# A graph layer with expert routing: two groups of seven node tiles in place of one of fourteen, and the first nodes' maxima moved behind them

## The chip, the cores and the metric

The kernel runs on one core of a Trainium2 chip. The metric is device time in microseconds (us), the median over repeated executions; lower is better. Five engines work side by side, each in the order of its own program: PE (matrix products; its weight loads are listed apart as PEld), DVE (vector operations), ACT (activations and copies; it also issues DMAs), POOL (here it issues the indirect DMAs, one row index per partition) and SP (it issues DMAs). They wait for each other and for transfers by semaphores.

## The reference, cut to what matters

There are 3125 nodes with 256 features (25 tiles of 128 nodes) and 100000 edges, sorted by destination. In outline:

```
xn  = layernorm(x)
a   = xn @ theta.T ;  b = xn @ (phi - theta).T          # per node
gnn = max over edges e of node d: relu(a[d] + b[src[e]] + biases)
mix = linear attention over all nodes: q (k^T v / N) w_out + b_out
x   = x + gnn + mix
# mixture of 8 experts, the best 2 of each node
x   = x + sum of 2: weight * (gelu(layernorm(x) @ W1[e]) @ W2[e])
```

All arithmetic is float32; an expert's two weight matrices are 2 MB together. Low node numbers have many edges: the 16 first nodes get a share of theirs by another way, told below.

## The kernel before, in words

**Head.** All 25 tiles are normalized and transposed, and `b` is written to a table in DRAM (L244 to L268). A search finds where each node's edges end.

**Edges.** The edges, from the highest node down, are laid out over 128 partitions and four stages of `STEPS` = 263, 209, 157 and 98 columns, 727 in all. For each column POOL issues one gather of 128 rows of `b` (L112, 1 KB a row) into a window of 8 columns; there are 5 windows (`wide`, `WN`). DVE folds column by column into a running maximum (`fold`, L387), and SP stores each finished window to a table `s_d` (L1487), after which the window can be filled again. A stage belongs to a group of node tiles: `GROUPS` = tiles 11 to 24, 4 to 10, 1 to 3, and 0.

**After a stage** (`group`, L1293): `carry` (L390) sends the last column through PE, a DVE scan and PE again, so that a run of edges that crosses partitions gets its maximum. Then for each tile POOL fetches the nodes' maxima from `s_d` (L416) and `token_tile` (L443) adds what belongs together, normalizes, and computes the routing logits on PE. `dispatch` (L1270) ranks the tokens and POOL scatters each tile twice to the experts' rows in `xs_d` (L119). Then the group joins the expert stream.

**Expert stream** (`Stream`, L682). A pass runs all 8 experts over a group. For tiles 11 to 24 every expert has room for `CAPS` = 512 rows, worked in two lots of 256; for tiles 4 to 10 it is one lot of 256, for tiles 1 to 3 one of 128. A lot is 8 steps of `hp` products (L645), a gelu on ACT (L647) and `yp` products (L669). Weights have three places; `plan` (L771) reuses those still there from the pass before and has ACT issue the others, in quarters of 512 KB between the steps. Tile 0 takes all its experts densely at the end (`dense_tile`), and `combine` (L1420) fetches the experts' rows back and writes the output.

**Work beside the edges.** `mixer` (L1163) handles one tile of the attention; 25 of them run under the first stage, after `turned` (L1100) has computed `b` transposed into `bT`. `without_edges` (L419) computes each tile's `a` and attention output. `first_nodes` (L1065) counts for each of the 16 first nodes which source nodes occur in the last 55 columns, and `first_maxima` (L1120) takes for each of them the maximum over all 25 tiles: PE spreads the node's mask (0 or -1e38) over 128 partitions into a PSUM bank (L1132), DVE adds it to `bT` and takes the maximum (L1136), for two halves of the features. It works on eight tiles (1024 columns) a step while the large bank is there, then on four (512) in a single bank that it shares with the expert stream.

**Order.** Every task is a Python generator; a clock that ticks once with each indirect DMA that POOL is given decides when its next piece is emitted, and `yield n` waits n ticks. PE, DVE, ACT and SP work in the order in which pieces were emitted. So a piece that comes late on one engine holds up everything emitted behind it there. `PER_TILE` and `PER_MIX` are the ticks between tiles. The mixers start at tick 16 but wait for `turned`, which starts at tick 30 and takes 21; `open_late` (L1246) frees the first part's memory and starts the expert stream, here at the end of the first stage's edges.

Of the kernel before, what the change touches and what calls it, by code (L numbers as in the profile page):

```python
# [8 lines left out]
F32 = mybir.dt.float32  # L9
# [25 lines left out]
ORDERS = ((0, 1, 2, 3, 4, 5, 6, 7), (6, 7, 5, 4, 0, 1, 2, 3), (2, 3, 1, 0, 4, 5, 6, 7))  # L35
# [6 lines left out]
GROUPS = ((11, 25), (4, 11), (1, 4), (0, 1))  # L42
STEPS = (263, 209, 157, 98)
CAPS = (512, 256, 128)
LOT = (256, 256, 128)
PARTS = (2, 2, 1)
# [14 lines left out]
PER_TILE = (5, 7, 4)  # L61
PACE = 0.9
# [10 lines left out]
def gps_layer(ctx: ExitStack, tc: tile.TileContext, x, src, dst, thetaT, phiT, gbias, wq, wkvT,  # L73
# [8 lines left out]
    clock = {"now": 0.0, "edges": 0, "tasks": 0, "pe": 0.0}  # L82

    def on_pe(us):
        clock["pe"] = max(clock["pe"], clock["now"]) + us / TICK

# [55 lines left out]
    bT = flat[:, 0:2 * NP].rearrange("p (h n) -> p h n", h=2)  # L142
    of_ring = ring.rearrange("p k n -> p (k n)")
    most = flat[:, 2 * NP:2 * NP + 2 * FIRST * CHUNKS].rearrange("p (h k c) -> p h k c", h=2, k=FIRST)
    ends_of = flat[:, 2 * NP + 2 * FIRST * CHUNKS:2 * NP + 2 * FIRST * (CHUNKS + 1)].rearrange("p (h k) -> p h k", h=2)
    halves = [of_ring[:, k * NP // 2:(k + 1) * NP // 2] for k in range(2)]
    no_edge = halves[1][0:FIRST].bitcast(BF16)
    unread = halves[0].bitcast(BF16)
# [39 lines left out]
    SPLIT = GROUPS[0][0]  # L188
    xn_lo = keep.tile([P, SPLIT, D], F32, name="xn_lo")
    xn_hi = keep.tile([P, NT - SPLIT, D], F32, name="xn_hi")  # L190
# [19 lines left out]
    row_of = keep.tile([FIRST, FIRST], BF16, name="row_of")  # L210
# [7 lines left out]
    nc.vector.tensor_copy(row_of, ident[0:FIRST, 0:FIRST])  # L218
# [171 lines left out]
    def carry(pool, ps, g, last, chain, carried):  # L390

        lt_p = ps.tile([P, 2, P], F32, name="mm")
        for c in range(2):
            nc.tensor.transpose(lt_p[:, c, :], last[:, c * P:(c + 1) * P], ident)
        on_pe(0.7)
        yield 3 if g < G - 1 else 1
        st = pool.tile([P, 2, P], F32, name="ct", bufs=2)
        for c in range(2):
            nc.vector.tensor_tensor_scan(st[:, c, :], through[:, g, :], lt_p[:, c, :],  # L399
                                         chain[0][:, c, P - 1:P] if chain else 0.0, op0=OP.add, op1=OP.max)  # L400
        chain[:] = [st]
        yield 2 if g < G - 1 else 1
        cr_p = ps.tile([P, D], F32, name="mm")
        for c in range(2):
            nc.tensor.transpose(cr_p[:, c * P:(c + 1) * P], st[:, c, :], ident)
        on_pe(0.7)
        yield 3 if g < G - 1 else 1
        cr = pool.tile([P, D + 1], F32, name=f"cr{g}", bufs=1)
        nc.vector.memset(cr[:, D:D + 1], 1.0)
        nc.vector.tensor_copy(cr[:, 0:D], cr_p)  # L410
        carried[g] = cr
# [7 lines left out]
    def without_edges(ps, i):  # L419

        am = ps.tile([P, 2 * D], F32, name="mm")
# [7 lines left out]
        nc.scalar.copy(x_sb[:, i, :], am[:, D:2 * D])  # L429

# [12 lines left out]
    def token_tile(work, ps, i, r1, slices, carried, top, top_i, newton=False, then=None,  # L443
# [56 lines left out]
        yield after(3)  # L500
        tr = ps.tile([P, 2, P], F32, name="mm")
# [5 lines left out]
        nc.scalar.copy(xtT, tr)  # L507
        yield after(2)
        lg = ps.tile([P, E], F32, name="mm")
# [6 lines left out]
        nc.vector.max_index(top_i, top, lg)  # L516

# [22 lines left out]
    def slots(ro, ps, g, half, i0, i1, pick, taken, chosen=None):  # L540
# [7 lines left out]
        if i1 == NT:  # L548
            nc.vector.tensor_scalar(took[:, nt - 1, :], took[:, nt - 1, :], real, None, op0=OP.mult)
        cnt_p = ps.tile([P, 2, nt, E], F32, name="mm")  # L550
# [20 lines left out]
        nc.vector.tensor_tensor(rank, cnt_p[:, 0], upto.rearrange("p e i -> p i e"), OP.add)  # L571

# [109 lines left out]
    class Stream:  # L682
# [9 lines left out]
        def add(self, g):  # L692
            self.lots += [(g, e, h) for e in ORDERS[g] for h in range(CAPS[g] // LOT[g])]

        def at_pair(self, u):

            g, e, h = self.lots[u]
            return h if CAPS[g] > LOT[g] else e % 2

        def half(self, u):  # L700

            g = self.lots[u][0]
            return LOT[g] // PARTS[g]

        def two(self, what, v):
# [3 lines left out]
            rows = what[g][e * CAPS[g]:e * CAPS[g] + 2 * LOT[g]]  # L709
            return rows.rearrange("(k p s) d -> p k s d", p=self.half(2 * v), k=2 * LOT[g] // CAPS[g])  # L710

        def at(self, to):

            return xn_hi[:, 4 * to:4 * to + 4, :]

        def as_two(self, rows, v):
            g = self.lots[2 * v][0]
            of = rows[0:self.half(2 * v), 0:2 * PARTS[g], :]
            return of.rearrange("p (k s) d -> p k s d", k=2 * LOT[g] // CAPS[g])
# [4 lines left out]
        def rows(self, v):  # L724
            if 2 * v < len(self.lots) and ("xs", v) not in self.held and not self.on_chip(2 * v):
                xs = self.held["xs", v] = self.at(v % 2)
                move(nc.scalar, self.as_two(xs, v), self.two(xs_d, v))
# [12 lines left out]
        def turn(self, u):  # L740
# [11 lines left out]
            elif ("xs", u // 2) in self.held and ("tr", u) not in self.held:  # L752
                tr = self.held["tr", u] = self.ps.tile([P, 2, ROWS], F32, name="trf", bufs=1)
                n = self.half(u)
                for c in range(2):
                    for r in range(2):
                        nc.tensor.transpose(tr[:, c, r * n:(r + 1) * n],  # L757
                                            self.held["xs", u // 2][0:n, self.at_pair(u) * 2 + r, c * P:(c + 1) * P],
# [3 lines left out]
        def scaled(self, u):  # L762
            if ("tr", u) in self.held and ("xe", u) not in self.held:
                e = self.lots[u][1]
                xe = self.held["xe", u] = self.act.tile([P, 2, ROWS], F32, name="xe")
                for c in range(2):
                    n = LOT[self.lots[u][0]]
# [30 lines left out]
        def more_w(self):  # L798
            while "firsts" not in clock:
                yield 1  # L800
            for k in (-2, -1):
                self.next_w(k)
                yield 25

        def go(self):
# [5 lines left out]
            while True:  # L811
                if u == len(self.lots):
# [3 lines left out]
                    units.behind = None  # L816
                    if not self.open:
# [13 lines left out]
                g, e, h = self.lots[u]  # L831
                v = u // 2
                if u % 2 == 0:
                    ys = self.at(2) if v % 2 else self.act.tile([P, 4, D], F32, name="ys", bufs=1)

                def done(r, yp, u=u, ys=ys):
                    g, e, h = self.lots[u]
                    n = self.half(u)
                    nc.tensor.matmul(yp[0:n, :], ident[0:E, e:e + 1].to_broadcast([E, n]), b2_sb, start=False, stop=True)  # L839
                    nc.scalar.copy(ys[0:n, self.at_pair(u) * PARTS[g] + r, :], yp[0:n, :])  # L840
                    if u % 2 and r == PARTS[g] - 1:
                        move(nc.scalar, self.two(ys_d, u // 2), self.as_two(ys, u // 2))
# [8 lines left out]
                if h == 0:  # L851
                    q += 1
                    if q:
                        between[7] = lambda q=q: (self.next_w(q, self.parts), self.part())
# [10 lines left out]
            dense_half(0, 1, xn_hi[:, 0:FC, :].rearrange("p i d -> p (i d)"), nc.scalar)  # L865
# [9 lines left out]
    def dense_tile(act, ps, mm, i, shared, w, next_w, order=range(E), ready=None):  # L875
# [5 lines left out]
        xT = act.tile([P, 2, P], F32, name="xT", bufs=1)  # L881
# [15 lines left out]
        o = act.tile([P, D], F32, name="o", bufs=1)  # L897
# [84 lines left out]
    p2 = early.enter_context(tc.tile_pool(name="p2", bufs=2, space=PSUM))  # L982
    column = ea.tile([P, FIRST * NT], I16, name="column")
# [4 lines left out]
    def loads():  # L988
# [19 lines left out]
        for g, cap in enumerate(CAPS):  # L1008
# [3 lines left out]
            n = LOT[g] // 2  # L1012
# [46 lines left out]
    def banks():  # L1059

        if "ffp" in at_hand:
            return 1, at_hand["ffp"].tile([P, 2, ROWS], F32, name="trf", bufs=1).rearrange("p c n -> p (c n)")
        return 2, p3.tile([P, 4 * ROWS], F32, name="banks")

    def first_nodes():  # L1065
# [10 lines left out]
        count_p = banks()[1][:, 0:FIRST * NT]  # L1076
# [9 lines left out]
        counts = ea.tile([P, FIRST, NT], F32, name="counts")  # L1086
        nc.scalar.copy(counts.rearrange("p k i -> p (k i)"), count_p)
        yield 2
        for i0 in range(0, NT, CHUNK):
            n = min(CHUNK, NT - i0)  # L1090
            rows_p = banks()[1][0:FIRST].rearrange("k (i p) -> k i p", p=P)
            for i in range(n):
                nc.tensor.transpose(rows_p[:, i, :], counts[:, :, i0 + i], ident)
            yield 2
            nc.vector.tensor_scalar(no_edge[:, i0 * P:(i0 + n) * P], rows_p[:, 0:n, :].rearrange("k i p -> k (i p)"), 0.5,
                                    NEG, op0=OP.is_lt, op1=OP.mult)
            yield 1
        start(first_maxima())

    def turned():  # L1100

        for i0 in range(0, NT, CHUNK):
            n = min(CHUNK, NT - i0)
            for h in range(2):
                bt_p = p2.tile([P, CHUNK, P], F32, name="k")
                for at, of, j, some in spans(i0, n):
                    for c in range(2):
                        nc.tensor.matmul(bt_p[:, at:at + some, :], wb[:, c, h * P:(h + 1) * P],  # L1108
                                         of[:, j:j + some, c * P:(c + 1) * P], start=(c == 0), stop=(c == 1))
                yield 1.5  # L1110
                nc.scalar.copy(bT[:, h, i0 * P:(i0 + n) * P], bt_p[:, 0:n, :].rearrange("p i n -> p (i n)"))
        clock["turned"] = True

    def spans(i0, n):

        low = max(0, min(n, SPLIT - i0))
        return [(at, of, j, some) for at, of, j, some in ((0, xn_lo, i0, low), (low, xn_hi, i0 + low - SPLIT, n - low))
                if some]

    def first_maxima():  # L1120

        nc.vector.memset(most, NEG)
        for k in range(FIRST):
            i0 = 0
            while i0 < NT:
                held, mask_p = banks()
                clock["bank"] = True
                tiles = min(held * CHUNK, NT - i0)
                n = tiles * P
                for at in range(0, n, CHUNK * P):  # L1130
                    to = min(n, at + CHUNK * P)
# [559 lines left out]
```

## Time and profile before

| | us |
|---|---|
| median of 14 runs (1697.84 to 1737.87) | 1711.21 |
| profiled execution | 1719.15 |
| its span, first to last instruction | 1717.3 |
| busy: PE / DVE / ACT / POOL | 1050.8 / 757.6 / 332.2 / 844.6 |
| 727 gathers of `b` on POOL (L112) | 702.9 |
| 723 folds on DVE (L387) | 349.1 |
| maxima of the first nodes on DVE (L1136): 78 of 1024 columns | 94.8 |
| the same: 36 of 512 columns | 24.5 |
| mean granted clock of PE, share of full | 0.752 |

Read it so: no engine is busy all the time, so the time is made of engines that wait for each other, stage by stage. "Granted clock" is the part of PE's full clock that the throttle left it. A row of the table by stage has the stretch, its length, and for each engine the busy time and the number of instructions; a row of the waits has who waited for what, the sum in us, how often, and the longest. "Remote" and "issue" stand for a release that the profile can't name.

### The profile page before, as it was taken

The numbers are of one execution on the slowest core, as the hardware profiler recorded it, in microseconds if no ns is written. First come the engines' busy times: TensorE is split into PE (matmuls) and PEld (weight loads), VectorE is DVE, ScalarE is ACT, GpSimd is POOL, SyncE is SP. The second block draws the span as 40 slices with busy tenths as digits, with TensorE's granted clock in tenths as the row PEclk, the third lists the DMA queues.
The fourth block names the chain that finished last, engine by engine and source line by source line (L and its number), as shares of the span: only waits on it lengthen the run. The fifth ranks groups of instructions, "written<-read, shape, count | busy, mean of one in ns | idle before, by whom it ended". The sixth has DMA issues, their size and how long they took to land.

```text
span 1717.3 us, 13741 instructions
## 1 busy us (share of the span) xinstructions
PE 1050.8 (61%) x4086; PEld 715.7 (42%) x4086; DVE 757.6 (44%) x2261; ACT 332.2 (19%) x796; POOL 844.6 (49%) x879
## 2 busy tenths in 40 slices
PE   3503866875584255731494996697025985479595
PEld 2401433332231133221373784575014864368484
DVE  3545776879559494323102103463331002515242
ACT  1300221221010121110121321221002322224131
POOL 6273573656645666377324434525771154631522
PEclk7755997887686555765696997788556996779696
DMA  7442663546446355255164654423651773549372
GB/s 234 154 148 77 232 230 129 184 164 204 160 146 238 120 204 187 92 202 165 51 216 132 230 197 153 153 111 138 205 187 37 250 236 101 196 138 354 121 268 79
DMA packets 93534, 292.88 MB, mean 171 GB/s; under 512 B 19398, under 2 KB 39871, under 8 KB 82698
## 3 DMA queue, kind: packets, MB, share of 16 engines
q0 software_dynamic: 42400, 115.28, 22.0%
q1 hardware_dynamic: 25420, 106.30, 16.0%
q10 hardware_dynamic: 25630, 70.34, 12.0%
q8 instruction: 34, 0.56, 0.1%
q14 instruction: 50, 0.41, 0.1%
HBM read 171.08 MB, written 120.75 MB: 170 GB/s over the span
## 4 chain that ended last, share of the span: by engine, by line
PE 40%; another core or an unknown queue 26%; DVE 15%; issue 14%; ACT 2%; DMA 2%; POOL 1%; ACTq 0%; DVEq 0%; SPq 0%; POOLq 0%
PE hp L645 12%; PE yp L669 11%; DVE g L387 4%; DVE ring L1136 2%; PE v L1168 2%; PE k L1168 2%; PE mm L424 2%; PE yp L839 2%; PE bp L262 2%; PE k L1108 1%; PE banks L1132 1%; ACT ring L647 1%; PE mm L422 1%; PE am L466 1%
## 5 line engine op out<-in xcount | busy, mean ns | idle before, releaser
L112 POOL DMA_INDIRECT g<-b_d,srcI x727 | 702.9, 967 | 544.6 <-issue 215.2
L387 DVE SCALAR_TENSOR_TENSOR g<-g,cut 128x256 f32<-128x256 f32 x723 | 349.1, 483 | 378.2 <-DMA g<-b_d,srcI 248.5
L647 ACT ACTIVATE ring<-hp,sm 128x256 f32<-128x256 f32 (+1 forms) x320 | 136.9, 431 | 582.9 <-PE hp L645 258.3
L645 PE MATMUL hp<-xe,big 128*128 128x256 f32 (+1 forms) x768 | 185.0, 368 | 74.0 <-issue 49.5
L645 PE MATMUL hp<-xe,w 128*128 128x256 f32 (+1 forms) x448 | 125.2, 414 | 169.8 <-issue 130.2
L645 PEld LDWEIGHTS hp<-xe,big 128*128 128x128 f32 x768 | 139.7, 205 | 103.1 <-issue 59.1
L669 PE MATMUL yp<-big,ring 128*128 128x256 f32 x624 | 177.1, 404 | 1.1 <-issue 1.1
L645 PEld LDWEIGHTS hp<-xe,w 128*128 128x128 f32 x448 | 90.3, 231 | 197.2 <-issue 142.3
L669 PEld LDWEIGHTS yp<-big,ring 128*128 128x128 f32 x624 | 120.7, 204 | 20.9 <-issue 6.2
L1136 DVE CUSTOM_DVE_ANT_0 ring<-big,banks 128x1024 bf16<-128x1024 f32 (+1 forms) x102 | 101.5, 996 | 57.4 <-remote 29.2
L669 PE MATMUL yp<-w,ring 128*128 128x256 f32 x368 | 106.7, 407 | 0.0
L669 PEld LDWEIGHTS yp<-w,ring 128*128 128x128 f32 x368 | 71.5, 205 | 12.3 <-issue 3.0
L112 POOL DMA_INDIRECT r<-s_d,end_i x25 | 23.6, 945 | 106.7 <-DMA s_d<-g 59.8
L112 POOL DMA_INDIRECT g<-ys_d,from_i x48 | 46.0, 958 | 55.0 <-DMA out<-g 24.1
L1132 PE MATMUL banks<-ring,row_of 16*128 16x512 bf16 (+1 forms) x90 | 30.8, 415 | 65.3 <-DVE big L1136 41.3
L399 DVE TENSOR_TENSOR_SCAN ct<-through,ct,mm 128x128 f32<-128x128 bf16 x6 | 2.6, 467 | 137.6 <-remote 137.6
L757 PE MATMUL trf<-ident,xn_hi 128*128 128x128 f32 x96 | 15.9, 292 | 60.9 <-DMA xn_hi<-xs_d 60.9
L1132 PEld LDWEIGHTS <-row_of 16*128 16x128 bf16 x112 | 7.8, 97 | 102.3 <-issue 53.3
L119 POOL DMA_INDIRECT xs_d<-xn_hi,slot_i x28 | 29.4, 1050 | 41.4 <-issue 40.5
L1132 PE MATMUL trf<-ring,row_of 16*128 16x512 bf16 (+1 forms) x22 | 11.5, 524 | 55.8 <-DVE big L1136 28.5
L466 PE MATMUL am<-cr,oh 128*128 128x257 f32 x82 | 35.4, 553 | 14.3 <-ACT kept L1417 11.3
L422 PE MATMUL mm<-bias,ones 1*128 1x512 f32 x50 | 32.6, 737 | 16.7 <-ACT x_sb L429 11.2
(316 smaller groups left out, 1428.9 us busy)
## 6 DMA issues: line engine op xcount, KB each, us to landing
s_d<-g SPq DMA_DIRECT2D x74, 1024.0 KB
big<-in_w ACTq DMA_DIRECT2D x36, 512.0 KB
s_d<-g SPq DMA_DIRECT2D x15, 896.0 KB
w<-in_w ACTq DMA_DIRECT2D x24, 512.0 KB
g<-b_d,srcI POOLq DMA_INDIRECT x727
big<-in_w ACTq DMA_DIRECT2D x4, 2048.0 KB
xn_hi<-xs_d ACTq DMA_DIRECT2D x12, 512.0 KB
xs_d<-zero ACTq DMA_DIRECT2D x8, 512.0 KB
```

What stands on the lines that cost most here:

```text
L112: got = nc.gpsimd.indirect_dma_start(out=to, out_offset=None, in_=table, in_offset=row_index(index))
L262: nc.tensor.matmul(bp, xnT(i, c), wb[:, c, :], start=(c == 0), stop=(c == 1))
L387: nc.vector.scalar_tensor_tensor(g[:, j, :], last, cut[:, t:t + 1], g[:, j, :], op0=OP.add, op1=OP.max)
L422: nc.tensor.matmul(am, ones[0:1, :], bias, start=True, stop=False)
L424: nc.tensor.matmul(am, xnT(i, c), am_w[:, c, :], start=False, stop=False)
L466: nc.tensor.matmul(r2, picks[k], carried[g], start=(k == 0), stop=(k == len(slices) - 1))
L645: nc.tensor.matmul(hp[:, 0:n], w1t[:, c, f, :], xe[:, c, 0:n], start=(c == 0), stop=(c == 1))
L647: nc.scalar.activation(hT[f][:, 0:n], hp[:, 0:n], AF.Gelu, bias=sm[:, 4 + f, e:e + 1])
L669: nc.tensor.matmul(yp[r][0:part, :], hT[q][:, r * part:(r + 1) * part], w2t[:, q, :], start=(q == 0), stop=(q == FC - 1 and self.whole))
L1132: nc.tensor.matmul(mask_p[:, at:to], row_of[:, k:k + 1].to_broadcast([FIRST, P]), no_edge[:, i0 * P + at:i0 * P + to], start=True, stop=True)
L1136: nc.vector.tensor_tensor_reduce(unread[:, 0:n], bT[:, h, i0 * P:i0 * P + n], mask_p[:, 0:n], 1.0, NEG, op0=OP.add, op1=OP.max, accum_out= ...
L1168: nc.tensor.matmul(to, xnT(i, c), wkv[:, c, k * INNER:(k + 1) * INNER], start=(c == 0), stop=(c == 1))
```

## The change

The first group is split in two, so that there are five stages and four passes through the expert stream instead of three:

```diff
-ORDERS = ((0, 1, 2, 3, 4, 5, 6, 7), (6, 7, 5, 4, 0, 1, 2, 3), (2, 3, 1, 0, 4, 5, 6, 7))
+ORDERS = ((6, 7, 5, 4, 0, 1, 2, 3), (2, 3, 1, 0, 4, 5, 6, 7)) * 2
-GROUPS = ((11, 25), (4, 11), (1, 4), (0, 1))
-STEPS = (263, 209, 157, 98)
-CAPS = (512, 256, 128)
-LOT = (256, 256, 128)
-PARTS = (2, 2, 1)
+GROUPS = ((18, 25), (11, 18), (4, 11), (1, 4), (0, 1))
+STEPS = (115, 148, 209, 157, 98)
+CAPS = (256, 256, 256, 128)
+PARTS = (2, 2, 2, 1)
-PER_TILE = (5, 7, 4)
+PER_TILE = (5, 6, 5, 4)
```

`turned` is gone, and the mixers wait for nothing:

```diff
     def mixers():
         yield 16
         mixer_weights()
-        while "turned" not in clock:
-            yield 1
...
         yield from mixer_product()
-        yield 2
-        for i in range(*GROUPS[0]):
-            start(without_edges(mm, i))
-            yield 3
+        yield 4
+        open_late()
+        for g in range(2):
+            for i in range(*GROUPS[g]):
+                start(without_edges(Early(), i))
+                yield 3.5 + g
```

`open_late` now comes here, after the mixers, and a group waits for it before its tiles. The weights of the first pass no longer wait for the first nodes' maxima. Those maxima start after the second group's dispatch, stop while any group has tiles in work, and take four tiles of `b` at a time, read back from the DRAM table into a gather window by SP and turned on PE:

```diff
+        clock.pop("tokens")
+        if g == 1:
+            start(rest_without_edges())
+            start(first_maxima())
...
+        def some(c):
+            rows = wide.tile([P, W, D], F32, name="g")
+            n = min(CHUNK, NT - c * CHUNK)
+            move(nc.sync, rows[:, 0:n, :], b_rows[:, c * CHUNK:c * CHUNK + n, :])
+            return rows
...
+            for h in range(2):
+                turned_p = late_bank[0]()
+                for i in range(n):
+                    nc.tensor.transpose(turned_p[:, i * P:(i + 1) * P], rows[:, i, h * P:(h + 1) * P], ident)
+                on_pe(0.28 * n)
+                yield 2
+                nc.scalar.copy(bT[:, h, 0:n * P], turned_p[:, 0:n * P])
...
+                if k == FIRST - 4 and c + 1 < CHUNKS:
+                    of_b[c + 1] = some(c + 1)
+                if k % 2 == 1:
+                    yield from seat()
+                mask_p = late_bank[k % 2]()
+                for i in range(n):
+                    at = k * NT + i0 + i
+                    nc.tensor.matmul(mask_p[:, i * P:(i + 1) * P], absent[:, at:at + 1].to_broadcast([P, P]), ident_h,
+                                     start=True, stop=True)
+                on_pe(0.1 * n)
+                yield 1.2
+                if held is not None:
+                    yield from seen(k - 1, held)
+                held = mask_p
```

`seen` is the two DVE operations of L1136, each over 512 columns (128 for the last tile), with `yield 0.2` behind each. The masks alternate between two banks, and a mask is emitted before the maximum of the one ahead of it. The mask comes from `absent` (128 sources by 16 x 25), so the transposes of the counts (L1093) and their ACT copy go. `seat` and `leave` count who holds one of the two general PSUM banks; a task that finds both taken looks again after 0.3 ticks. It is used in `carry`, `token_tile`, `slots`, `without_edges`, `last_ends` and `verdict` as well.

In the expert stream every lot is now one expert of one group; an expert's result goes out with a store of its own instead of one store for two lots. Some scratch memory moves: the mixers' temporaries into the second half of `big`, `bT` and `most` into free parts of `xn_hi`.

## Prediction

> **What bounds the kernel now.** I read the table by stage first, cut where the work changes: head of the edges, mixers, rest of stage one, its 14 tiles, its expert pass, stage three beside that pass, stage four, tail.
>
> ```profile
> core 0: us, PE busy (x) PEld busy (x) DVE busy (x) ACT busy (x) POOL busy (x), PEclk, DMA share, GB/s
> 73.00:196.00 123.00, 38.58 (x130) 20.47 (x131) 69.34 (x268) 7.29 (x13) 76.40 (x77) 0.62 0.47 157
> 196.00:404.00 208.00, 155.91 (x468) 72.72 (x466) 159.66 (x352) 47.94 (x101) 115.55 (x118) 0.86 0.52 176
> 404.00:518.00 114.00, 71.58 (x177) 30.83 (x178) 76.28 (x167) 10.30 (x31) 66.16 (x69) 0.73 0.52 179
> 518.00:752.00 234.00, 109.78 (x276) 52.92 (x274) 137.76 (x497) 34.04 (x85) 136.13 (x139) 0.58 0.48 166
> 752.00:981.00 229.00, 139.29 (x531) 104.69 (x532) 55.79 (x115) 42.61 (x93) 106.61 (x112) 0.75 0.49 164
> 981.00:1368.00 387.00, 252.81 (x1017) 197.59 (x1016) 118.19 (x401) 78.28 (x177) 171.61 (x178) 0.78 0.47 158
> 1368.00:1557.00 189.00, 125.24 (x605) 102.21 (x605) 56.65 (x196) 47.73 (x108) 92.14 (x96) 0.80 0.53 181
> 1557.00:1717.00 160.00, 119.97 (x689) 104.57 (x688) 52.13 (x147) 40.67 (x112) 51.63 (x54) 0.83 0.57 199
> ```
>
> The POOL column counts its indirect DMAs; I call each a call. Length by calls gives 1.60, 1.76, 1.65, 1.68, 2.04, 2.17 and 1.97 us a call for the seven stages of edges. Undisturbed, POOL makes 86 calls from 725 to 835 us, 1.27 each. So POOL paces the kernel but is held up everywhere, most where experts run beside edges (2.04, 2.17). No other engine is full there. The waits say by what:
>
> ```profile
> POOL g L112 <- DMA s_d<-g: 157.9, 5, 59.4
> ...
> SPq L105 <- DMA w<-in_w: 136.4, 6, 88.9
> ...
> DVE ct L399 <- remote: 137.6, 3, 62.8
> ```
>
> POOL waits for a window's store; SP, which stores, waits (once for 88.9 us) for weight transfers that ACT issues between expert steps; DVE's scan in `carry` waits for PE transposes emitted behind expert steps. All three are late because PE is behind its plan. Why, two rows of PE and three of ACT tell:
>
> ```profile
> 929.00:1030.00 101.00, 98.07 (x430) 78.10 (x429) 7.75 (x16) 31.86 (x71) 34.80 (x37) 0.97 0.61 209
> ...
> 1202.00:1310.00 108.00, 17.41 (x41) 10.82 (x41) 37.37 (x77) 4.96 (x12) 71.87 (x75) 0.52 0.50 165
> ```
>
> ```profile
> 1270.22 0.47 ACT L647 ACTIVATE ring<-hp,sm 128x256 f32<-128x256 f32 x1 [10.73 <-remote]
> ...
> 1281.42 0.47 ACT L647 ACTIVATE ring<-hp,sm 128x256 f32<-128x256 f32 x1 [10.73 <-remote]
> 1292.62 0.47 ACT L647 ACTIVATE ring<-hp,sm 128x256 f32<-128x256 f32 x1 [10.73 <-remote]
> ```
>
> Dense, PE makes 430 products in 101 us, so a lot (64 products and some 6 small ones) takes 16.4 us. But from 1202 to 1297, while POOL calls without a pause, one gelu starts every 11.2 us, and PE makes 41 products in 108 us; 752 to 845 is alike. When POOL stops, PE runs. So edges and experts partly take turns, the 16 lots of the first pass need 752 to 1202, 450 us instead of 262, and stage three pays.
>
> **The change, part by part.** I count in calls, since the order is written in them, and cut where pieces are emitted: mixers from 16, 25 x 5, then 12 + 23 + 4, so `open_late` at call 180; stage two's edges end at 263 + 21 (7 fetches, 14 scatters of tiles 18 to 24) = 284; tiles 11 to 17 are scattered by about 365; stage three's edges end at 514, stage four's at 692, the last at 793. Head to call 0: 73 us, as before.
>
> *Calls 0 to 180.* Before, call 181 starts at 369.8, so 297 us. `turned` goes (33 us of PE from 162 to 192, before the first mixer), and the mixers start 35 calls earlier. The first maxima leave: 50 of DVE's 125 us from 242 to 404 (162 us), and 14 of PE's 119. That stretch was full at 77% DVE and 73% PE; what is left of PE, 104, at 73% gives 143 us instead of 162, 19 saved. But the mixers now meet `first_nodes` (32 us of DVE) earlier. I take 275; ends 250 (1.27 a call and the 20.7 us stall there) and 297.
>
> *180 to 284*, 104 calls: 14 `without_edges`, seven tiles, scatters, 6 MB of weights. Before: 404 to 752, 348 us for 208 calls, 1.67; 79 of DVE's 214 us there are first maxima and go. I take 1.5, 156 us; ends 1.27 and 1.67, 132 and 174.
>
> *284 to 365*, 81 calls: tiles 11 to 17 beside the first pass, as tiles 4 to 10 are now, 94 calls in 212 us (981 to 1193), 2.25. That gives 182; the low end, 1.67, 135.
>
> *365 to 514*, 149 calls: second pass, 11 `without_edges`, first maxima. Those become 16 x 7 steps of two operations, 680 ns and 82 each (280 for the last tile): 158 us of DVE instead of 140. A step is 1.6 ticks, so DVE needs 1.52 + 1.6 x 0.483 = 2.30 us a step, 1.43 a call: more than POOL's 1.27. At the 80% that DVE reaches (160 of 208 us under the mixers): 1.8 a call, 268 us. Ends: 1.27, 189; and 2.4, 358, from the single bank's phase, 22 steps in 91 us (537 to 628), 4.1 a step. I am nearer the low end because two banks alternate. PE: 400 mask products of 128 columns; 512 columns take 0.44 us, a 128-column float32 transpose 0.29, so 0.11 to 0.29, I take 0.15, 60 us, and 50 transposes, 15 us. With eight lots (131) that fits into 268. ACT: 14 copies of 0.585, as `turned` had.
>
> *514 to 692*, 178 calls: seven tiles with no experts beside them, 75 x 1.67 = 125; 60 calls of first maxima at 1.8, 108, beside the third pass; 43 x 1.67, 72. Sum 305 against 387; ends 1.5 and 2.17 a call, 267 and 387. Here most is won: the eight lots before it fit into the 268 us above, while today 8 of the first pass's 16 lots are still to do at 981 (264 of its 512 `hp` products).
>
> *692 to 793*: 189 now, of which 42 (to 1410) still see the previous pass. I take 180; ends 150, 189. *Tail*: unchanged, 160.
>
> *Weights*: 23 expert loads instead of 18, five more of 2 MB, all beside edges: 20 quarters. The rows price them through POOL's waits for stores, 158 us over 40 quarters loaded beside edges now, 3.9 each, so 0 (PE in time) to 79. I take 30. *Read back*: seven SP loads, 3.3 MB; each can hold the stores behind it until its window's store has landed (at 2 MB in 10 us, some 5 us), 0 to 35, with four windows as cover; 0 taken, and if the cover goes it shows as POOL waiting on stores. Sixteen more result stores: 16 x 0.33 on ACT, under PE. `seat` emits nothing; tiles use 1.4 of two seats, so it moves little.
>
> Sum: 73 + 275 + 156 + 182 + 268 + 305 + 180 + 160 + 30 = 1629, with 2 outside the span 1631. The profiled execution had 1719.15, so -88; from the median 1711, that is **1623**.
>
> **A page against it.** PE's granted clock was 0.97 in the dense row and 0.52 in the sparse one; four `hp` products took 2.07 us in the latter. The Trainium skill, "TensorE: Matmul & The Clock Gate", section "HAM oscillation — how this bites in real kernels", states that PE idle for more than some 3.4 us falls back to half clock, and the change strews its lots thinner. By that rule alone the 16 lots of two passes would take about twice 262 us, an estimate from that page's halving; the measured 450 us already hold such stretches, so I add nothing.
>
> **Rivals.**
> *First maxima bind (slower).* Place: calls 365 to 514 and 595 to 655. DVE waits in order for a mask emitted behind expert steps, and PE's answers come on an 11.2 us grid when POOL is undisturbed. For it: the single bank's 4.1 us a step, DVE over POOL's pace even by need. Against: two banks; and a held DVE holds POOL, which frees PE. Price, over the 1.6 x 1.8 = 2.88 us taken: 112 x (4.1 - 2.88) = 137, so 1760. It decides from 2.88 + 88/112 = 3.7 us a step.
> *Turns only.* Edges and experts exclude each other whenever they are emitted, so that an earlier start wins nothing. For it: the 11.2 us grid. Against: from 1030 to 1202 both move. Then calls 284 to 692 take what they take now, 554 to 1368, 814 us instead of 755, and the next stage its 189: 1691. That the change does not do what it says comes to the same.
> *All slack is used.* Stages after 284 at 1.5: 408 x 1.5 = 612 instead of 755, and no weights' 30: about 1450 at best; with half of that, 1537. Against: no stage of before with tiles in it went below 1.6.
>
> **Numbers.** Forecast (1560 to 1680) 0.43; all slack 0.10; turns only (1680 to 1720) 0.14, of which 0.10 is faster, 0.03 the same and 0.01 slower; first maxima bind 0.33, of which 0.01 ends the same. Two medians of this kernel can be told apart from about 0.3%, 5 us, so "same" is 1706 to 1716. Faster 0.43 + 0.10 + 0.10 = 0.63, same 0.04, slower 0.33. The range leaves out 0.1 on each side: 1540, where half the slack is used, to 1760, where the first maxima bind at the single bank's rate.
>
> **What would show it.** First mixer before 120 us and call 180 by 350; call 514 near 920 and 692 near 1230; fewer than 60 us of POOL's waits on window stores; first maxima at 2.9 us a step. I am wrong if DVE's waits for masks exceed 100 us in sum, or if SP's waits for weights grow beyond today's 136 us, or if stage two's edges end after 518.

## The result, and the profile after

The changed kernel takes **9373.72 us** (median of 10 runs, 9363.28 to 9403.21) against 1710.59 for the kernel before on the same chip: ratio 5.492, 95% interval 5.477 to 5.507. Neither the forecast of 1623 nor its range nor any rival held it.

The page of after tells where the time is, in its rows over 40 slices of 234 us each (tenths of a slice):

```profile
span 9369.6 us, 46108 instructions
...
PE   4457666100000000000000000032001877777777
...
POOL 5544454014444444204444444477775000000000
...
DMA  4544565100000000000000000055555555555444
```

Seven slices look like the kernel before. Then PE all but stands still for some twenty slices, in most of which POOL works, and at the end PE works without POOL. The table of two stretches and the timeline of SP at their border (start, duration, engine, line, what) show that these are two programs, one behind the other:

```profile
0.00:1691.00 1691.00, 1033.24 (x4385) 736.70 (x4385) 794.87 (x2577) 322.81 (x784) 846.80 (x879) 0.77 0.53 181
1691.00:9370.00 7679.00, 1858.98 (x10297) 1592.66 (x10297) 1392.69 (x2975) 724.21 (x1874) 2341.64 (x2397) 0.61 0.23 84
```

```profile
1689.48 0.35 SPq L112 DMA_DIRECT2D out<-xn_hi  x1
1691.06 0.35 SPq L1573 DMA_DIRECT2D raw<-in_dst  x1
```

At 1689.48 the last rows of the output are stored: the kernel of the diff has done its work. 1.6 us later the edge list is read afresh from the inputs. The costliest group and the largest transfers of the page name what runs from there on:

```profile
L126 POOL DMA_INDIRECT rec_d<-rec,posI x1564 | 1519.0, 971 | 2870.2 <-DMA rec_d<-rec,posI 2186.4
...
w<-in_w SPq DMA_DIRECT2D x200, 2048.0 KB
```

1564 scatters sort the edges, and 200 loads of 2 MB take all 8 experts' weights past each of 25 tiles. That is the **general path**, which stands at the end of both kernels behind a test (L1539 before):

```
        nc.vector.tensor_scalar(over, rank, float(cap), None, op0=OP.is_ge)
...
        nc.vector.tensor_tensor(lost, over, took, OP.mult)
        nc.vector.tensor_reduce(bad[:, ...], lost.rearrange("p i e -> p (i e)"), AX.X, OP.add)
...
    wrong = nc.values_load(odd[0:1, 0:1])
    with tc.If(wrong > 0), ...
```

`dispatch` gives each token a rank among those that chose the same expert. A rank at or over `CAPS` has no row in `xs_d`; it is counted in `bad`, `verdict` sums that into `odd`, and if the sum isn't zero everything is computed again by a way that has no capacities.

The fast part alone, by the stages of the prediction:

```profile
core 0: us, PE busy (x) PEld busy (x) DVE busy (x) ACT busy (x) POOL busy (x), PEclk, DMA share, GB/s
72.00:195.00 123.00, 49.74 (x159) 25.94 (x159) 82.31 (x293) 11.88 (x25) 75.08 (x77) 0.71 0.45 149
195.00:385.00 190.00, 107.38 (x348) 58.65 (x348) 109.78 (x245) 38.59 (x79) 101.94 (x106) 0.79 0.54 186
385.00:566.00 181.00, 88.07 (x223) 43.83 (x222) 72.65 (x256) 26.95 (x68) 102.29 (x104) 0.68 0.54 191
566.00:737.00 171.00, 113.71 (x451) 87.27 (x450) 64.91 (x276) 36.19 (x82) 77.62 (x81) 0.77 0.49 161
737.00:1030.00 293.00, 216.88 (x925) 150.27 (x926) 151.20 (x424) 52.86 (x125) 144.25 (x149) 0.80 0.54 185
1030.00:1363.00 333.00, 189.23 (x860) 147.53 (x858) 171.57 (x613) 55.49 (x127) 173.20 (x179) 0.75 0.53 181
1363.00:1542.00 179.00, 113.09 (x557) 93.68 (x558) 59.14 (x205) 38.09 (x94) 96.41 (x100) 0.76 0.54 184
1542.00:1691.00 149.00, 118.95 (x669) 100.80 (x667) 51.97 (x148) 39.53 (x109) 47.77 (x50) 0.86 0.58 207
```

Per call that is 1.79, 1.74, 2.11, 1.97, 1.86 and 1.79 us from the second row to the seventh. Before, it was 1.6 to 1.8 ahead of the experts and 2.0 to 2.2 beside them. The jam is spread, not gone. What the waits of the fast part say:

```profile
DVE xn_hi L1125 <- PE am L1146: 73.0, 9, 45.8
DVE xn_hi L1125 <- remote: 70.8, 10, 19.6
...
DVE ct L407 <- PE mm L402: 52.8, 1, 52.8
...
POOL g L119 <- DMA s_d<-g: 48.3, 7, 28.1
...
SPq L112 <- DMA big<-in_w: 36.1, 4, 12.2
```

POOL's waits for window stores fell from 157.9 to 48.3 us and SP's largest row of waits for weights from 136.4 to 36.1, the first as forecast. DVE now waits for the masks of the first nodes (L1125), 144 us in two rows.

### The profile page after: what moved, and what is told of

Read it like the earlier page. It is cut to its first block, busy times and chain, and to the rows that moved or that the text cites. A ratio compares the mean times of both kernels' runs of the same rounds, so it can differ in the third digit from the quotient of the medians.

```text
span 9369.6 us, 46108 instructions
## 1 busy us (share of the span) xinstructions
PE 2892.2 (31%) x14682; PEld 2329.4 (25%) x14682; DVE 2187.6 (23%) x5551; ACT 1047.0 (11%) x2658; POOL 3188.4 (34%) x3276
## 3 DMA queue, kind: packets, MB, share of 16 engines
q14 instruction: 127, 1.04, 0.0%
## 4 chain that ended last, share of the span: by engine, by line
DMA 44%; PE 22%; issue 14%; DVE 10%; another core or an unknown queue 4%; DVEq 4%; POOL 2%; ACT 1%; ACTq 0%; SPq 0%; POOLq 0%
DMA rec_d<-rec,posI 35%; PE hp L666 12%; DMA w<-in_w 8%; PE yp L690 7%; DVEq L394 4%; DVE run L1614 2%; DVE g L394 2%; POOL g L119 1%; DVE run L1615 1%; DVE pos L1616 1%; DVE eq L1612 1%; DVE num L1596 0%; PE am L481 0%; PE v L1179 0%
## 5 line engine op out<-in xcount | busy, mean ns | idle before, releaser
L126 POOL DMA_INDIRECT rec_d<-rec,posI x1564 | 1519.0, 971 | 2870.2 <-DMA rec_d<-rec,posI 2186.4
L119 POOL DMA_INDIRECT g<-b_d,srcI x1509 | 1477.5, 979 | 808.5 <-issue 454.2
L666 PE MATMUL hp<-xe,w 128*128 128x128 f32 (+1 forms) x6848 | 1140.6, 317 | 462.8 <-DMA w<-in_w 375.4
L666 PEld LDWEIGHTS hp<-xe,w 128*128 128x128 f32 x6848 | 1074.5, 222 | 567.3 <-issue 385.4
L394 DVE SCALAR_TENSOR_TENSOR g<-g,cut 128x256 f32<-128x256 f32 x1503 | 727.1, 484 | 772.0 <-DVE g L394 355.8
L690 PE MATMUL yp<-w,hT 128*128 128x256 f32 x3200 | 830.7, 382 | 0.0
L668 ACT ACTIVATE hT<-hp,sm 128x128 f32<-128x128 f32 x1600 | 587.0, 368 | 1257.5 <-PE hp L666 1220.4
L690 PEld LDWEIGHTS yp<-w,hT 128*128 128x128 f32 x3200 | 555.1, 194 | 41.3
L900 DVE TENSOR_SCALAR xe<-xT,sm 128x128 f32<-128x128 f32 x400 | 120.6, 344 | 1389.9 <-PE hp L666 1389.8
L1614 DVE TENSOR_TENSOR_SCAN run<-all,base,eq 128x782 f32<-128x782 f32 x114 | 209.1, 1836 | 0.1
```

The lines of the kernel that those rows point to most:

```text
L119: got = nc.gpsimd.indirect_dma_start(out=to, out_offset=None, in_=table, in_offset=row_index(index))
L126: put.append(nc.gpsimd.indirect_dma_start(out=table, out_offset=row_index(index), in_=of, in_offset=None))
L394: nc.vector.scalar_tensor_tensor(g[:, j, :], last, cut[:, t:t + 1], g[:, j, :], op0=OP.add, op1=OP.max)
L666: nc.tensor.matmul(hp[:, 0:n], w1t[:, c, f, :], xe[:, c, 0:n], start=(c == 0), stop=(c == 1))
L668: nc.scalar.activation(hT[f][:, 0:n], hp[:, 0:n], AF.Gelu, bias=sm[:, 4 + f, e:e + 1])
L690: nc.tensor.matmul(yp[r][0:part, :], hT[q][:, r * part:(r + 1) * part], w2t[:, q, :], start=(q == 0), stop=(q == FC - 1 and self.whole))
```

## The experiments

Sixteen kernels ran, each against the kernel before on the same chip; ratios are to that kernel. "Flag off" means the edit of the first experiment.

**1. Is it the overflow, and of how many rows?** In the changed kernel alone, the second group (tiles 11 to 17) counts a token as lost from rank 257 on, not 256:

```diff
-        nc.vector.tensor_tensor(lost, over, took, OP.mult)
+        if g == 1:
+            nc.vector.scalar_tensor_tensor(lost, rank, 257.0, took, op0=OP.is_ge, op1=OP.mult)
+        else:
+            nc.vector.tensor_tensor(lost, over, took, OP.mult)
```

> The changed kernel with one comparison altered: for tiles 11 to 17 a token counts as lost only from the 258th row of an expert on (limit 257 in place of 256). Rows past 256 still go to the dump rows, so if there is a 257th, that token leaves out one expert's share. Theory 'one row too many': the general path runs only because some expert of tiles 11 to 17 gets exactly 257 rows; then the flag stays 0 and the time is that of the first 1690 us of the profile after and what lies around it, 1690 to 1700 us. Rival 'another guard' (order of the edges, a border of the new stages, tiles 18 to 24): the flag stays set, 9374 us. Rival 'many rows': two or more rows over, 9374 us as well.

Measured: 1738.03 us against 1734.8, ratio 0.9985 (0.994 to 1.003). So one row too many is enough: an expert of tiles 11 to 17 gets exactly 257 rows of 256, none gets more, and no other group loses any. Without the general path the change is worth nothing that can be measured.

The kernel before with its first group's limit lowered, by the same edit with `g == 0` and 491:

> The kernel before with the same comparison tightened for its first group: a token counts as lost from an expert's 492nd row on (limit 491 in place of 512). Nothing else is changed. If the general path is the whole of the loss and costs the same here, the time is 1711 + (9374 - 1692) = about 9390 us, provided that an expert of tiles 11 to 24 gets 492 rows or more, as the two halves' counts suggest. If the loss comes from the change itself, 1711 us.

Measured: 9508.35 us (a single run), against 1734.8 without. So the price, some 7770 us, is that of the general path and has nothing to do with the change; and an expert of tiles 11 to 24 gets at least 492 rows of 512.

Other borders of the groups, nothing left out (`...` at the end stands for two small changes of storage that follow from them):

```diff
-GROUPS = ((18, 25), (11, 18), (4, 11), (1, 4), (0, 1))
-STEPS = (115, 148, 209, 157, 98)
-CAPS = (256, 256, 256, 128)
-PARTS = (2, 2, 2, 1)
-SPLIT = 11
+GROUPS = ((19, 25), (12, 19), (5, 12), (1, 5), (0, 1))
+STEPS = (97, 143, 196, 193, 98)
+CAPS = (256, 256, 256, 160)
+PARTS = (2, 2, 2, 2)
+SPLIT = 12
...
```

> The changed kernel with other borders: groups of tiles 19 to 24, 12 to 18, 5 to 11, 1 to 4 and 0; stages of 97, 143, 196, 193 and 98 columns; the fourth group's experts have room for 160 rows in two parts of 80 instead of 128. Nothing is left out. Theory 'one row too many': with these borders no expert runs over, no general path, 1690 to 1720 us: the fourth pass is a quarter longer at the end (60 of 240 hp and yp row units, about 14 us) and has one tile more. Rival 'another guard': 9370 us or so.

> The kernel with the other borders once more, nothing left out, on the chip of this call. A gain that belongs to the order holds: 0.980 to 0.993, as the 0.9872 measured before. If it is of one chip only, the interval here reaches 1.00.

Measured: 0.9872 (0.9822 to 0.9923), and on a second chip 0.9892 (0.9847 to 0.9938). With borders one tile further up no expert overflows, and the kernel is 1.1 to 1.3% faster than the one before. This is the version that beats both kernels. How much of it is due to the split and how much to the borders is not separated: with the old borders and the flag off the split gave 0.9985.

**2. Does an early first pass win time?** Flag off, the first group's lots join the stream only with the second group's:

```diff
-        at_hand["ffn"].add(g)
+        if g == 1:
+            at_hand["ffn"].add(0)
+        if g > 0:
+            at_hand["ffn"].add(g)
```

> The altered kernel of the first run (limit 257), but the first group's lots join the expert stream only together with the second group's, so that the first pass starts about 95 calls later, as in the kernel before; all work is the same. Prediction on record (an early first pass gives slack): 40 to 80 us slower than the first run. 'Turns only' (edges and experts exclude each other, an early start wins nothing): within 15 us of the first run.

Measured: 0.9926 (0.9877 to 0.9975), against 0.9985 (0.994 to 1.003) with the early pass. The intervals overlap: late is not slower. The same edit with the other borders:

> The other borders of the groups, with which no expert overflows, and the first group's pass begun only with the second group's: nothing is left out. Apart they gave 0.9872 and 0.9926 (against 0.9985 of the split kernel with its flag off), so if the two savings are of different stages they add to 0.980 to 0.983. If both only remove the same jam in the second pass, it stays at 0.987 or above.

Measured: 1.0293 (1.0177 to 1.0408, 4 runs). Expected was 0.980 to 0.983 if the two savings add, and 0.987 or above if both remove the same jam; that it would be slower than the kernel before was not foreseen. Call 692 came at 1342 us, earlier than the 1356 with the early pass, but from there to the end took 405 us, not 358; PE was busy for 324 us of that, not 257, with 1595 products, not 1306. The lots that were put off had to be done in the last stages. So the start of a pass moves the jam about; that its sign depends on how much PE work is left for the end is a reading of these two profiles, not shown apart.

**3. Do the first nodes' maxima bind?** They are set to -1e38 and all their work is left out, in the split kernel (flag off) and in the one before:

```diff
-            start(first_maxima())
+            nc.vector.memset(of_first, NEG)
+            clock["firsts"] = True
```

> The first nodes' maxima are left out of the split kernel (they are set to -1e38), with its flag off as in the run with one row more. Its ratio there was 0.9985. Theory 'turns only': edges and experts exclude each other, the maxima fill DVE's and PE's gaps, and the ratio falls by less than 0.015, to 0.984 or more. Rival 'first maxima bind': the 112 steps took what the earlier pass won, some 88 us, so the ratio falls by 0.04 or more, to 0.96 or less; the prediction's own price, 2.88 us a step of which 1.27 a call would run anyway, lies between.

> The first nodes' maxima are left out of the kernel before (set to -1e38). Both theories of the split need this as a zero: 'turns only' expects that they cost the kernel before as much as the split one, within 0.01 of the ratio. 'First maxima bind' expects that they cost less here, since 78 of the 114 steps of before take 1024 columns at once under the mixers: a ratio of 0.98 or more, against 0.96 or less in the split kernel.

Measured: 1.006 (1.0019 to 1.0102) and 1.0053 (1.0017 to 1.009). Without 112 us or more of DVE's work both kernels are no faster. "First maxima bind" is out, though DVE waits 144 us for the masks: whoever waits there has nothing better to do. In the stage that holds most of them, calls 365 to 514, the split kernel takes 299 us without them and 293 with them (one profiled execution each, flag off). In the kernel before the edit also lets the weights of the first pass come earlier, since they wait for the maxima there.

**4. Do the weight loads bind?** Only the first three experts' weights are loaded:

```diff
-                self.held["w", k] = load_w(self.wts[k], e, nc.scalar, parts)
+                if parts is None:
+                    self.held["w", k] = load_w(self.wts[k], e, nc.scalar, parts)
```

> Only the first three experts' weights are loaded in the split kernel (flag off); every later expert computes with what lies in its place, so 20 of 23 expert loads of 2 MB are left out. If the extra loads ate the gain (prediction: 30 us for five, at most 79, so 6 to 16 us a load), the ratio falls by 0.07 or more for all twenty, to 0.93 or less. If weights hide behind the turns of edges and experts, it stays at 0.98 or more.

> The same in the kernel before: only the first three experts' weights are loaded, 15 of 18 loads of 2 MB are left out. What the five further loads of the split kernel cost is its fall less this one's. Loads that bind: 0.95 or less here (6 to 16 us a load over 15), and 0.02 to 0.05 less again in the split kernel. Loads that hide: 0.985 or more in both.

Measured: 0.9983 (0.9952 to 1.0015) in the split kernel, that is nothing for 40 MB less, and 1.0258 (1.0196 to 1.0321) in the one before, which got slower: a miss of both theories. In its profile calls 365 to 514 take 268 us, not 303, and calls 514 to 595 take 258, not 184. Why is open; what is shown is that the loads do not hold the kernel up.

**5. Does PE's work bind?** Of the 8 parts of each second product only two are computed:

```diff
+                if q in (0, FC - 1):
-                nc.tensor.matmul(yp[r][0:part, :], hT[q][...], w2t[:, q, :], start=(q == 0), ...
+                    nc.tensor.matmul(yp[r][0:part, :], hT[q][...], w2t[:, q, :], start=(q == 0), ...
```

> The experts' second product is cut in the split kernel (flag off): of its 8 parts per half lot only the first and the last are computed, so some three quarters of the 290 us of yp products, about 215 us of PE, are left out; the order of emission is the same. If edges and experts take turns, so that a lot costs its own PE time, the ratio falls by 0.06 or more, to 0.94 or less. If the pace beside the experts is set by the answers' grid and by waits in order, not by PE's work, it falls by less than 0.03, to 0.97 or more.

> The same cut of the second product in the kernel before, some 215 us of PE left out. Turns: 0.94 or less. Grid and waits in order: 0.97 or more. If the split kernel gains more by the cut than this one, its narrower passes had PE as their bound; if less, they had not.

Measured: 0.9615 (0.9534 to 0.9696) in the split kernel, which lies between the two theories; 1613.45 us against 1712.03 before, a ratio of medians of 0.942 (4 runs, 1592 to 1631, no interval; the two fastest against the five fastest of before give 0.937). PE's busy time fell by only 154 us (1043.2 to 889.1) and 136 us (1050.8 to 915.3): in the kernel before the second products went from 284 to 88 us, but at a mean clock of 0.71, not 0.75, the others took longer. The time fell by 63 and by 99 to 108 us: 0.4 and 0.7 to 0.8 of each us of PE.

**6. Do POOL's calls bind?** Every second gather is left out, and the fold takes the column before once more, so that DVE, PE, ACT and SP do what they did:

```diff
+            other = last if j % 2 else g[:, j, :]
-            nc.vector.scalar_tensor_tensor(g[:, j, :], last, cut[:, t:t + 1], g[:, j, :], op0=OP.add, op1=OP.max)
+            nc.vector.scalar_tensor_tensor(g[:, j, :], last, cut[:, t:t + 1], other, op0=OP.add, op1=OP.max)
...
-                gather(wins[g, w][:, j, :], b_d[:], srcI[:, t:t + 1])
+                if j % 2 == 0:
+                    gather(wins[g, w][:, j, :], b_d[:], srcI[:, t:t + 1])
```

> Every second gather of b is left out in the split kernel (flag off), and the fold of such a column takes the column before it once more, so DVE works as before; some 360 of 794 calls on POOL are gone at an unchanged order of emission. If POOL's calls pace the whole, 1.27 us each undisturbed, up to 460 us go, a ratio near 0.75. If calls wait for the chain of DVE, PE and ACT anyway (1.6 to 2.2 us a call measured), the ratio stays over 0.90.

> Every second gather left out in the kernel before, as in the split one, where it gave a ratio of 0.7465. If calls pace both kernels alike, 0.73 to 0.77. If the wide first pass of before has PE as its bound once POOL has time, so that here the split would pay, it stays at 0.78 or above.

Measured: **0.7465** (0.736 to 0.7571) in the split kernel and 0.7857 (0.7797 to 0.7917) in the one before. 357 and 356 calls went; by the ratios (0.9985 - 0.7465 of 1712, 1 - 0.7857 of 1731) 431 and 371 us, 1.21 and 1.04 us a call. That is nearly what a call takes when POOL runs without a pause (1.27 in the prediction's view), though POOL was busy for half the span only. Two rows show it, the stretch from the first call to near the end, first the split kernel with its flag off, then with half its gathers:

```profile
72.00:1549.00 1477.00, 860.57 (x3372) 591.33 (x3372) 698.80 (x2277) 251.82 (x578) 757.29 (x780) 0.75 0.51 173
```

```profile
72.00:1180.00 1108.00, 864.76 (x3818) 619.42 (x3819) 727.56 (x2382) 278.02 (x648) 442.40 (x451) 0.86 0.60 208
```

PE does its work, and more products than before, in 369 us less: it is busy for 78% of the stretch instead of 58%, at a granted clock of 0.86, not 0.75. ACT's waits for the products of PE behind which the profile sees nothing, in the same two kernels (sum, times, longest):

```profile
ACT ring L671 <- remote: 322.0, 40, 26.1
```

```profile
ACT ring L672 <- remote: 88.6, 17, 11.2
```

With half the calls 233 us of these 322 are gone: with fewer gathers PE's answers come sooner. That a gather itself slows them is one reading, and not the only one. At 1.27 us each, the 780 calls of the first row take 991 of its 1477 us and leave 486; the 451 calls of the second take 573 of 1108 and leave 535. The 369 us won are thus less than the 418 that the missing calls take by themselves, so it would also do if POOL's calls lay in series with what POOL waits for, stage after stage. No run tells the two apart. What is shown is that the time follows the number of calls, though POOL's busy share is one half.

**7. Calls or bytes?** Flag off, all folds take the column before, and the gathers fetch half a row (then, as a control, a whole one):

```diff
-                gather(wins[g, w][:, j, :], b_d[:], srcI[:, t:t + 1])
+                if t == COL[g]:
+                    gather(wins[g, w][:, j, :], b_d[:], srcI[:, t:t + 1])
+                else:
+                    gather(wins[g, w][:, j, 0:D // 2], b_d[:].rearrange("n (h d) -> (n h) d", h=2), srcI[:, t:t + 1])
```

> In the split kernel (flag off) every gather but the first of a stage fetches rows of 512 B in place of 1 KB, and the folds take the column before it in place of the gathered one: as many calls, rows and folds, half the gathered bytes (some 47 MB of 307 MB less). If the others pay for bytes, this gives about half of what leaving out half the gathers gave, which halved the bytes too: a ratio near 0.85 to 0.90. If they pay for calls, it stays within 0.02 of its control with whole rows.

> The control of the run with half rows: the folds take the column before in place of the gathered one, the gathers are whole. Both theories expect what the split kernel with its flag off had, 0.99 to 1.01; a fold still waits for its gather, since it writes over it.

Measured: 1.0033 (0.9976 to 1.0091) with half rows, 0.9895 (0.9828 to 0.9961) with whole ones. Half the gathered bytes bring nothing; the control (4 runs) was even 1.4% faster. What is paid for is the call, or its 128 rows, not what they carry. The Trainium skill, "DMA: Bandwidth & Descriptors", section "SWDGE vs HWDGE vs iDMA", says that software on POOL's cores computes one pair of descriptors per operation before any byte moves; that agrees with this pair of runs. Whether and how a call holds PE's answers up, neither the page nor a run here tells.

## Why the prediction was wrong

**The step that failed** is in "The change part by part": the prediction took "mixers", "weights", "read back" and "`seat`" each in turn, and of the line `CAPS` 512 to 256 only that 16 lots become twice 8. It never asked how many rows an expert gets. The one sentence that could have led there, "that the change does not do what it says comes to the same", put this at 1691 us, while the kernel has a test with a price of 7770 us behind it. In its place the runs showed that tiles 11 to 17 send 257 rows to an expert with 256 places. The inputs are fixed, so that number could have been counted beforehand: by the reference's own routing, tiles 11 to 17 send 257 rows to expert 4 and 253 to expert 1, and tiles 18 to 24 send at most 239 to one. With the borders one tile further up the fullest expert of these two groups has 255 rows, so that version too fits by a single place.

It could also have been feared without counting. Tile 24 holds only 53 nodes, so tiles 11 to 24 are 1717 tokens and send 1717 x 2 / 8 = 429 rows to an expert on average, with 83 places to spare; tiles 11 to 17 are 896 tokens and send 224, with 32. The mean is nearly the same share of the capacity, but the scatter of a count falls only by the root: if tokens chose by lot, sqrt(1717 x 0.25 x 0.75) = 17.9 rows before, sqrt(896 x 0.25 x 0.75) = 13.0 after. The spare places fall from 4.6 to 2.5 times the scatter. Halves don't pool. The fullest expert of the kernel before had 492 of its 512 rows taken; it is expert 1, with 253 and 239 in the two halves, and these fit. Expert 4, with 465, looked safer, but 257 of them lie in one half.

**The fast part**, step by step (calls as in the prediction; us):

| calls | forecast | ends | after | before |
|---|---|---|---|---|
| head | 73 | | 72 | 73 |
| 0 to 180 | 275 | 250, 297 | 312 | 297 |
| 180 to 284 | 156 | 132, 174 | 182 | 185 |
| 284 to 365 | 182 | 135, 182 | 171 | 124 |
| 365 to 514 | 268 | 189, 358 | 293 | 303 |
| 514 to 692 | 305 | 267, 387 | 333 | 387 |
| 692 to 792 | 180 | 150, 189 | 179 | 194 |
| tail | 160 | | 148 | 155 |
| five loads, and outside | 32 | 0, 79 | 0 | |
| sum | 1631 | | 1690 | 1718 |

- *Calls 0 to 284* missed by 37 and 26 us, and only these two stretches lie outside their ends. The first mixer came at 110 us, before 120 as forecast, but call 180 at 385, not by 350. The gain was worked out from what DVE and PE no longer do there. The kernel before without its maxima tells what that is worth, against three profiled executions with them (the one above, and those of experiments 4 and 5, which do the same up to call 284): calls 0 to 180 take 288 us, against 287 to 297, so little was to be won there; calls 180 to 284 take 147, against 177 to 185, so that gain was real. It is given back at once: the next 81 calls take 179, against 124 to 125. The split kernel doesn't get even that far, with 312 and 182. What the prediction left out is the price of what the split puts there in exchange: by call 115 it is at 212 us behind the head, against 178 to 185, with its mixers beside `first_nodes`. Which of the new pieces costs this, no run separates.
- *Calls 365 to 514*: the steps of the maxima were nearly right in size. 130 of the 224 operations, 65 steps, ran from 816 to 1030 us, 3.3 us a step (2.9 was forecast, and 3.7 was the point from which they should bind), and the stage took 293 us, inside its ends. But the steps were not what it waited for, since the stage is as long without them (299 us).
- *Calls 514 to 692*, "most is won": 54 us were won, of 82, inside the ends.
- *Five extra loads*: 30 taken, the lower end was right; leaving out twenty loads brought nothing.
- *What would show it*: POOL's waits on stores are under 60 us and SP's for weights under 136, as forecast, and still the gain stayed away; DVE's waits for masks are over 100 us, which was a sign of being wrong by the first rival, and they cost nothing. These three were waits, and none of them set the pace. The sign that told was a time: stage two's edges ended at 566 us, after 518.
- "Turns only" was the nearest for the fast part (0.9985 of before with the flag off), but that its 1691 us meets the 1690 here is luck: it took the forecast's gain in calls 0 to 284, which failed by 63 us, and was too high by 17 in calls 284 to 692, by 10 in the next stage, by 12 in the tail and by the 30 for weights. What it claimed as its mechanism is half shown: fewer gathers bring PE's answers sooner, and a cut of PE's work shortens the time by 0.4 to 0.8 of it, as it would if the two took turns in part. "An earlier start wins nothing" doesn't hold in general, since with the other borders a late pass cost 4%. With half the gathers the split kernel is 4 points faster than the one before (0.7465 against 0.7857), some 68 us, near the 88 that were forecast: with fewer calls the split pays. That this is the forecast's own gain, for its own reason, is not shown.

## What to carry to other kernels

When a change makes a buffer smaller that data decide how to fill, count the fullest case before anything is timed, and look up what the kernel does when it overflows; two halves of a capacity don't hold what the whole held. Where no engine is full, a wait's length is not what it costs: leave work out of each engine once and see which one the time follows, here the number of POOL's calls and, in part, PE's products. POOL's busy share of one half hid that each gather left out saved 1.04 to 1.21 us of the whole; smaller rows saved nothing.

## What was not expected of the hardware

While POOL calls without a pause, PE's answers come late and in steps. In the kernel before, the profile has eight products done at 1248.44 + 3.78 = 1252.2 us, and the gelu that needs the first of them starts 6.8 us later, though ACT was free:

```profile
1248.44 3.78 PE L645 MATMUL hp<-xe,w 128*128 128x256 f32 x8 [3.42 <-issue]
...
1259.02 0.47 ACT L647 ACTIVATE ring<-hp,sm 128x256 f32<-128x256 f32 x1 [10.18 <-issue]
```

This and the next gelus, at 1270.22, 1281.42 and 1292.62, stand 11.2 us apart, which is neither a window of eight calls (10.2 us at 1.27) nor the length of nine (11.24 to 11.32 us in this stretch), nor that of any product here. It is not the weight loads either, which ACT issues: in the kernel before without them, gelus still start at 791.00, 802.21, 813.41 and 824.60 us. The step is there in single waits of after too, but longer ones, to 26.1 us with the flag off, hide it; in the split kernel with half the calls 11.2 us was the longest. What makes the step was not found.

The granted clock follows how dense PE is: 0.75 in the stretch with all gathers, 0.86 with half, with the same kinds of products in both. The Trainium skill, "TensorE: Matmul & The Clock Gate", section "HAM oscillation — how this bites in real kernels", has pauses of over some 3.4 us bring the clock down, and the two rows agree in direction. So a pause that the calls make may cost a second time, in slower products behind it; how much of the time won is due to the clock, no run separates.
